# The start of an attention kernel: q and k positions as row part plus column part, x loaded first, idle products in the first gaps

## The chip, the cores and the metric

The kernel runs on one NeuronCore of one Trainium2 chip. The metric is the time of one execution on the device, in microseconds, as a median of several runs. A core has five engines with queues of their own: PE (TensorE, matrix products into PSUM), DVE (VectorE), ACT (ScalarE), POOL (GpSimd) and SP (SyncE, here only a queue of transfers). They run side by side and wait for one another through semaphores. 16 DMA engines move data between memory and SBUF.

## The reference, cut to what matters

The input x is 8 images of 128 channels and 48 x 48 = 2304 positions. Two layers follow each other. The first is a causal attention over the positions of the group-normalised x; the second a full attention over the same tokens, and a feed-forward recurrence. The change lies in the projections of the first layer:

```python
pe = jnp.broadcast_to(_pos_embeddings(S)[None], (B, 2 * EMB, S, S))
x0 = jnp.concatenate([x, pe], axis=1).reshape(B, C + 2 * EMB, N)     # C = 128, EMB = 16, N = 2304
q = lrelu(jnp.einsum('kc,bcn->bkn', Wq, x0) + bq[None, :, None])
k = lrelu(jnp.einsum('kc,bcn->bkn', Wk, x0) + bk[None, :, None])
v = lrelu(jnp.einsum('vc,bcn->bvn', Wv, x0) + bv[None, :, None])
attn = jnp.einsum('bkn,bkm->bnm', q, k) / jnp.sqrt(jnp.float32(Kdim))
# ... causal mask, softmax, times v; then x + this, layer norm, full attention, feed-forward
```

The 32 position channels are the same for all images. 16 of them depend on the row of the image alone and 16 on its column alone (`px`, `py` in `_pos_embeddings`). So W applied to them, plus the bias, is one fixed table of 128 x 2304 for each of q, k and v, and for each position a sum of a term by row and a term by column.

## The kernel before

All arithmetic is float32. The 2304 positions are cut into six chunks of QC = 384. A chunk n of an image is projected so: DVE normalises x (`xn`), PE multiplies by the three weights (`pj`), DVE adds the position table (`z`) and takes the leaky relu (`q`, `k`, `vT`), and reduces q and k to their largest magnitudes (a bound for the softmax). The position table `pb` of a chunk is made in the first image: PE multiplies the 33 position rows (32 channels and ones) by their weights, ACT copies the result from PSUM, and it is stored to memory (`posb_d`), from where later uses load it. In the first image chunks 0 and 1 are used straight from where they are made, chunks 2 to 5 are loaded back.

The engines' orders are fixed by the program. Chains of steps (`st.add`) are put between the attention products by a small model of the engines' times in the program: `tick` runs the steps that it holds ready, `advance` and `finish` force a chain to a step. The start and the projections:

```python
load_x(0, 3)                        # three transfers of 128x768 on the SP queue
...
wT = apool.tile([P, 3, P], F32, tag="wT", name="wT")
pe_sb = [gpool.tile([P, N // 2], F32, tag="g", name=f"pe_{h}") for h in range(2)]
wpT = tpool.tile([P, N // 2], F32, tag="t", name="wpT")[:, : 3 * P].rearrange("p (j c) -> p j c", j=3)
nc.scalar.dma_start(wpT[: NPE + 1], w_pos)
nc.scalar.dma_start(pe_sb[0][: NPE + 1, :], pe[:, : N // 2])
nc.scalar.dma_start(wT, w_qkv)
nc.sync.dma_start(pe_sb[1][: NPE + 1, :], pe[:, N // 2 :])
nc.sync.dma_start(w1, w_ffn)
...
def positions(n, j):                # table of chunk n for q, k, v (j = 0, 1, 2)
    if j == 0:
        if n < 2:
            pos[0, n] = made[n] = pbp.tile([P, 3, QC], F32, tag="pb", name=f"pb_0_{n}")
        else:
            made[n] = tpool.tile([P, 3 * QC], F32, tag="t", name=f"pb_0_{n}").rearrange("p (j c) -> p j c", j=3)
    pe_c = pe_sb[n // (NQ // 2)][: NPE + 1, ts(n % (NQ // 2), QC)]
    ps = psum_s(f"pb_{n}_{j}")
    if j < 2:
        nc.tensor.matmul(ps[:, :QC], wpT[: NPE + 1, j, :], pe_c, start=True, stop=True)
    else:
        for m in range(0, QC, P):
            nc.tensor.matmul(ps[:, ds(m, P)], pe_c[:, ds(m, P)], wpT[: NPE + 1, j, :], start=True, stop=True)
    nc.scalar.copy(made[n][:, j, :], ps[:, :QC])
    if j == 2:
        nc.sync.dma_start(posb_d[:, n], made[n])
...
def project(b, n):
    def normed():
        if n > 1:
            st.finish(projected[b, n - 2])
        if (b, n) in pos_loads:
            st.finish(pos_loads[b, n])
        c["pb"] = pos.pop((b, n))
        ...
        nc.vector.tensor_scalar(c["xn"], xbuf[b][:, cols], mg, rs, ALU.subtract, ALU.mult)
    def part(j):
        def f():
            ps = psum_s(f"pj_{b}_{n}_{j}")
            ...                     # q, k: one product of 384 columns; v: three of 128
            z = chunk_tile("z", f"z_{b}_{n}_{j}")
            nc.vector.tensor_add(z, ps[:, :QC], c["pb"][:, j, :])
            ...
            nc.vector.scalar_tensor_tensor(dst, z, 0.01, z, ALU.mult, ALU.max)
            if j == 2:
                for i in range(2):
                    nc.vector.tensor_reduce(
                        largest[b][:, i, n : n + 1], c[i], AX.X, ALU.max, apply_absolute_value=True
                    )
                load_positions(*divmod(b * NQ + n + 2, NQ))
                if n + 1 < EARLY:
                    project(b, n + 1)
    steps = [(normed, 0.0, [("DVE", 0.75)])]
    steps += [(part(j), QC * US, [("DVE", 0.0 if j < 2 else 4.5)]) for j in range(3)]
...
idle(psum_s("idle"), 12)            # 12 products of 128 columns that nobody reads
for j in range(3):
    positions(0, j)
gn = st.add(group_norm(0))          # statistics (DVE), mean and variance over groups (PE, DVE), root (POOL)
st.advance(gn, 2)
positions(1, 0)
st.finish(gn)
for j in range(1, 3):
    positions(1, j)
project(0, 0)
making = st.add([(partial(positions, n, j), QC * US, [("ACT", 0.5)]) for n in range(2, NQ) for j in range(3)], 6.0)
```

After that the attention products follow: for each query chunk j and key block m a score `s` (keys as weights, 384 columns or less), its exponential `p` on ACT (the block on the diagonal masked by POOL), and three scores later its product with v into `o`, while DVE adds p up into `acc`. `psum_s` has four buffers, `tpool` and `pbp` two each.

Of the kernel before, what the change touches and what calls it, by code (L numbers as in the profile page):

```python
# [21 lines left out]
EMB = 16  # L22
# [10 lines left out]
def position_rows(side):  # L33
# [13 lines left out]
    return np.ascontiguousarray(np.concatenate([px, py, ones], axis=0).reshape(NPE + 1, side * side))  # L47

# [556 lines left out]
def fast_path(ctx: ExitStack, tc: tile.TileContext, x, pe, w_ffn, out, x_tok, w_qkv, w_pos, v_t, gamma_beta, flag):  # L605
# [58 lines left out]
    with ExitStack() as actx:  # L664
# [69 lines left out]
        wpT = tpool.tile([P, N // 2], F32, tag="t", name="wpT")[:, : 3 * P].rearrange("p (j c) -> p j c", j=3)  # L734
        nc.scalar.dma_start(wpT[: NPE + 1], w_pos)
        nc.scalar.dma_start(pe_sb[0][: NPE + 1, :], pe[:, : N // 2])
        nc.scalar.dma_start(wT, w_qkv)
        nc.sync.dma_start(pe_sb[1][: NPE + 1, :], pe[:, N // 2 :])
# [4 lines left out]
        def ffn_weights():  # L743
# [4 lines left out]
            nc.vector.tensor_scalar(w1, w1, s, None, ALU.subtract)  # L748
            tp = psum_t("tp_ffn")
# [68 lines left out]
        keys, vals, queries, largest, projected = {}, {}, {}, {}, {}  # L818

        pos, pos_loads, made = {}, {}, {}  # L820

        def positions(n, j):

            if j == 0:
                if n < 2:
                    pos[0, n] = made[n] = pbp.tile([P, 3, QC], F32, tag="pb", name=f"pb_0_{n}")
                else:
                    made[n] = tpool.tile([P, 3 * QC], F32, tag="t", name=f"pb_0_{n}").rearrange("p (j c) -> p j c", j=3)
            pe_c = pe_sb[n // (NQ // 2)][: NPE + 1, ts(n % (NQ // 2), QC)]
            ps = psum_s(f"pb_{n}_{j}")  # L830
            if j < 2:
                nc.tensor.matmul(ps[:, :QC], wpT[: NPE + 1, j, :], pe_c, start=True, stop=True)  # L832
            else:
                for m in range(0, QC, P):
                    nc.tensor.matmul(ps[:, ds(m, P)], pe_c[:, ds(m, P)], wpT[: NPE + 1, j, :], start=True, stop=True)
            nc.scalar.copy(made[n][:, j, :], ps[:, :QC])
            if j == 2:
                nc.sync.dma_start(posb_d[:, n], made[n])

        def load_positions(b, n):  # L840
            def f():
                if b == 0:
                    st.advance(making, 3 * (n - 1))
# [3 lines left out]
            if b < B:  # L847
                pos_loads[b, n] = st.add([(f, 0.0, [])], st.free["DVE"] - st.now)

        def project(b, n):  # L850
# [4 lines left out]
            def normed():  # L855
                if n > 1:
                    st.finish(projected[b, n - 2])
                if (b, n) in pos_loads:
                    st.finish(pos_loads[b, n])
                c["pb"] = pos.pop((b, n))  # L860
# [8 lines left out]
            def part(j):  # L869
                def f():  # L870
# [15 lines left out]
                    if j == 2:  # L886
                        for i in range(2):
                            nc.vector.tensor_reduce(
                                largest[b][:, i, n : n + 1], c[i], AX.X, ALU.max, apply_absolute_value=True
# [743 lines left out]
```

## Time and profile before

| | |
|---|---|
| time, median of 3 runs | 1772.9 us (1772.55 to 1773.56) |
| span of the profiled execution | 1772.5 us |
| instructions | 22223 |
| moved by DMA | 262.00 MB, 148 GB/s on average |

A page of the profile gives the busy time of each engine (PEld is PE's weight load, which overlaps PE), the chain of work that ended last, and groups of instructions by line. An answer of the trace gives single instructions in order of time: when each began, how long it took, how long its engine had been idle before it and what released it. A float32 product appears in the records as two instructions (x2 for one product, x6 for three). In a product's operands the first number is of rows times columns of the weights: `33*128` is a position product, which has 33 rows, `128*128` one that uses the whole array. Idle time of an engine costs nothing as long as another engine sets the pace at that moment.

### The profile page before, as it was taken

Reading aid. Unit: us, or ns where it says so; the run is one execution under the profiler, and the core shown is the slowest. Engines: PE = TensorE matmul, PEld = TensorE weight load, DVE = VectorE, ACT = ScalarE, POOL = GpSimd, SP = SyncE. Lnnn points to the kernel's source line nnn. Section 1 sums busy time; section 2 is a strip of 40 time slices with the busy share of each in tenths; the row PEclk is TensorE's granted clock in tenths of the full one; section 3 lists DMA queues with packets and bytes.
Section 4 is the critical chain, followed back from the end, with each engine's and each line's share of the span. In section 5 each row is a group of like instructions: output and inputs, shape, how many; then the busy total and the mean of one; then the engine's idle time right before and its main releaser. Section 6 shows DMA issues by size and latency. Waiting matters only on the chain.

```text
span 1772.5 us, 22223 instructions
## 1 busy us (share of the span) xinstructions
PE 1742.7 (98%) x6231; PEld 1093.2 (62%) x6231; DVE 1302.8 (74%) x3363; ACT 764.8 (43%) x1842; POOL 195.2 (11%) x303
## 2 busy tenths in 40 slices
PE   8999999999999999999999999999999999999996
PEld 5666566665666566665666656665666656665565
DVE  4868668876887668786687767876687866877467
ACT  2344434443345434444344433454344543444455
POOL 1110011100110001100111001100011001110006
PEclk8999999999999999999999999999999999999998
DMA  4405672257533584156732575335941468116768
GB/s 140 138 23 187 182 204 94 87 184 188 145 103 128 159 226 141 34 176 182 200 99 80 188 192 152 106 111 161 237 129 50 160 183 214 45 65 198 194 211 216
DMA packets 206056, 262.00 MB, mean 148 GB/s; under 512 B 90113, under 2 KB 175010, under 8 KB 205412
## 3 DMA queue, kind: packets, MB, share of 16 engines
q1 hardware_dynamic: 204972, 257.47, 49.4%
q0 software_dynamic: 720, 2.62, 1.0%
q8 instruction: 52, 0.85, 0.2%
q14 instruction: 80, 0.66, 0.1%
q10 hardware_dynamic: 232, 0.40, 0.1%
HBM read 150.24 MB, written 110.17 MB: 147 GB/s over the span
## 4 chain that ended last, share of the span: by engine, by line
PE 96%; DMA 1%; DVE 1%; ACT 0%; issue 0%; SPq 0%; POOL 0%; ACTq 0%; POOLq 0%; DVEq 0%
PE o L1228 18%; PE s L1214 18%; PE s L1013 17%; PE o L1024 17%; PE o L1224 13%; PE pj L874 4%; PE pj L877 2%; PE z L1547 2%; PE wx L1320 2%; PE of_t L934 1%; PE tb L934 1%; PE pb L832 0%; DMA x<-in_x_dram 0%; PE dn L1072 0%; PE ts L1259 0%
## 5 line engine op out<-in xcount | busy, mean ns | idle before, releaser
L1216 ACT ACTIVATE p<-s,shift 128x384 f32<-128x384 f32 x504 | 292.4, 580 | 479.7 <-PE s L1214 464.2
L1015 ACT ACTIVATE p<-s 128x384 f32<-128x384 f32 (+2 forms) x504 | 231.8, 460 | 424.8 <-PE s L1013 377.5
L1214 PE MATMUL s<-xh 128*128 128x384 f32 x1008 | 410.4, 489 | 0.0
L1228 PE MATMUL o<-p,xhT 128*128 128x384 f32 x1008 | 404.1, 488 | 5.9 <-ACT p L1216 5.9
L1013 PE MATMUL s<-q,k 128*128 128x384 f32 (+2 forms) x1008 | 381.5, 460 | 0.2 <-DVE k L884 0.2
L1024 PE MATMUL o<-p,vT 128*128 128x384 f32 (+2 forms) x1008 | 377.4, 456 | 0.0
L1224 PE MATMUL o<-g,xhT 128*128 128x384 f32 x720 | 281.3, 488 | 1.1 <-DMA g<-e 1.1
L1228 PEld LDWEIGHTS o<-p,xhT 128*128 128x128 f32 x1008 | 188.9, 190 | 133.8 <-ACT p L1216 10.5
L1024 PEld LDWEIGHTS o<-p,vT 128*128 128x128 f32 x1008 | 188.8, 190 | 114.7 <-issue 0.6
L1214 PEld LDWEIGHTS s<-xh 128*128 128x128 f32 x1008 | 186.2, 190 | 115.3
L1013 PEld LDWEIGHTS s<-q,k 128*128 128x128 f32 x1008 | 182.6, 191 | 97.3 <-issue 1.0
L1039 DVE TENSOR_TENSOR acc<-acc,p 128x384 f32<-128x384 f32 (+2 forms) x408 | 208.8, 512 | 33.4 <-POOL p L1018 8.7
L1177 DVE STREAM_TRANSPOSE t<-p 128x384 f32<-128x384 f32 x360 | 187.3, 550 | 37.6 <-ACT p L1216 32.8
L1224 PEld LDWEIGHTS o<-g,xhT 128*128 128x128 f32 x720 | 133.2, 190 | 83.7 <-DMA g<-e 1.3
L1185 DVE TENSOR_REDUCE tsum<-t 128x12 f32<-128x1152 f32 x120 | 162.3, 1353 | 4.2
L879 DVE TENSOR_TENSOR z<-pj,pb 128x384 f32<-128x384 f32 x144 | 78.8, 547 | 108.8 <-PE pj L874 92.4
L1018 POOL TENSOR_TENSOR p<-p,triu 128x128 f32<-128x128 f32 x144 | 72.5, 505 | 606.2 <-ACT p L1015 475.2
L1294 POOL TENSOR_TENSOR roots<-ve_f,mhalf 128x3 f32<-128x3 f32 x48 | 40.7, 849 | 521.8 <-DVE ve_f L918 521.8
L1216 ACT ACTIVATION_READ_ACCUMULATOR p<-s,shift 128x1 f32 x504 | 97.2, 193 | 0.0
L874 PE MATMUL pj<-xn,wT 128*128 128x384 f32 x192 | 79.7, 500 | 1.4 <-DVE xn L867 1.4
L924 POOL TENSOR_TENSOR rs_c<-ve_c,mhalf 128x3 f32<-128x3 f32 x48 | 45.1, 939 | 216.2 <-DVE ve_c L918 213.6
L1321 DVE TENSOR_TENSOR scale<-wx,scale 128x384 f32<-128x384 f32 x46 | 25.4, 551 | 56.1 <-PE wx L1320 50.3
(264 smaller groups left out, 1485.6 us busy)
## 6 DMA issues: line engine op xcount, KB each, us to landing
e<-t SPq DMA_DIRECT2D x120, 576.0 KB
g<-e SPq DMA_DIRECT2D x480, 144.0 KB
pb<-posb_d SPq DMA_DIRECT2D x46, 576.0 KB
t1t<-in_x_tok_dram SPq DMA_DIRECT2D x48, 192.0 KB
t_d<-tt SPq DMA_DIRECT2D x184, 48.0 KB
t2x<-t_d SPq DMA_DIRECT2D x46, 192.0 KB
scale<-rs SPq DMA_DIRECT2D x46, 192.0 KB
x<-in_x_dram SPq DMA_DIRECT2D x14, 576.0 KB
```

What stands on the lines that cost most here:

```text
L874: nc.tensor.matmul(ps[:, :QC], wT[:, j, :], xn, start=True, stop=True)
L879: nc.vector.tensor_add(z, ps[:, :QC], c["pb"][:, j, :])
L1013: nc.tensor.matmul(s[:, off:QC], keys[b][:, ts(m, P)], queries[b, j][:, off:], start=True, stop=True)
L1015: nc.scalar.activation(p[:, off:], s[:, off:QC], AF.Exp, scale=SCALE)
L1024: nc.tensor.matmul(o[:, off:QC], vals[b][:, ts(m, P)], p[:, off:], start=first, stop=last)
L1039: nc.vector.tensor_add(a[:, off:], a[:, off:], p[:, off:])
L1177: nc.vector.transpose(t[:, :, :, g, :].rearrange("p b j r -> p j b r"), p.rearrange("p (j b r) -> p j b r", j=QB, b=R))
L1185: nc.vector.tensor_reduce(self.tsum[j][:, n - j - 1, :], t.rearrange("p b j m r -> p (b j) (m r)"), AX.X, ALU.add)
L1214: nc.tensor.matmul(s[:, :QC], xh[:, ts(m, P)], xh[:, ts(j, QC)], start=True, stop=True)
L1216: nc.scalar.activation(p, s[:, :QC], AF.Exp, bias=shift, accum_out=self.rows[:, m, j : j + 1])
L1224: nc.tensor.matmul(out_ap, xhT[:, QB * i + g, :], p, start=first, stop=last)
L1228: nc.tensor.matmul(o[:, :QC], xhT[:, what[1], :], p, start=first, stop=last)
```

## The change

The term by row and the term by column are made once for q and k (two products of 96 columns, copied by ACT). POOL adds them for every position of a chunk, with two broadcast operands, so that PE and ACT no longer make these two thirds of the table. The third for v, which needs the positions as rows, is made as before. In the first image every chunk is used where it is made; the store to memory stays, for the later images. x comes ahead of the large weight and position loads: on the ACT queue only two small loads are left, and the rest stand behind x on the SP queue. Idle products, 9, 4 and 5 of them, stand on PE where it waits for x and for the two steps of the statistics, to keep its clock up. The two maxima of a chunk become a chain of their own, and the preparation of a feed-forward weight is cut in two steps and moves from 30 to 60 us of the program's model of time. The core of the diff (cut: the new argument `pe_rc` in signatures and inputs):

```diff
@@
     py = np.broadcast_to(t[:, None, :], (EMB, side, side))
 ...
     return np.ascontiguousarray(np.concatenate([px, py, ones], axis=0).reshape(NPE + 1, side * side))
+def position_parts(side):
+    rows = position_rows(side)
+    parts = np.zeros((NPE + 1, 2, side), np.float32)
+    parts[:EMB, 0], parts[NPE, 0] = rows[:EMB, ::side], 1.0
+    parts[EMB:NPE, 1] = rows[EMB:NPE, :side]
+    return parts
 ...
 @with_exitstack
@@
 ...
         pe_sb = [gpool.tile([P, N // 2], F32, tag="g", name=f"pe_{h}") for h in range(2)]
-        wpT = tpool.tile([P, N // 2], F32, tag="t", name="wpT")[:, : 3 * P].rearrange("p (j c) -> p j c", j=3)
+        SIDE = pe_rc.shape[-1]
+        rcs = gpool.tile([P, N // 2], F32, tag="g", name="rcs")
+        rc_sb = rcs[:, : 2 * SIDE]
+        wpT = rcs[:, 6 * SIDE : 6 * SIDE + 3 * P].rearrange("p (j c) -> p j c", j=3)
         nc.scalar.dma_start(wpT[: NPE + 1], w_pos)
-        nc.scalar.dma_start(pe_sb[0][: NPE + 1, :], pe[:, : N // 2])
-        nc.scalar.dma_start(wT, w_qkv)
-        nc.sync.dma_start(pe_sb[1][: NPE + 1, :], pe[:, N // 2 :])
+        nc.scalar.dma_start(rc_sb[: NPE + 1, :], pe_rc.rearrange("k i s -> k (i s)"))
+        nc.sync.dma_start(wT, w_qkv)
+        for h in range(2):
+            nc.sync.dma_start(pe_sb[h][: NPE + 1, :], pe[:, ts(h, N // 2)])
         nc.sync.dma_start(w1, w_ffn)
 ...
-        def ffn_weights():
+        def ffn_centred():
 ...
             nc.vector.tensor_scalar(w1, w1, s, None, ALU.subtract)
+        def ffn_turned():
             tp = psum_t("tp_ffn")
 ...
             nc.vector.tensor_copy(w1T, tp[:, 0:P])
@@
             return [(part1, 0.0, [("DVE", 3.6)]), (part2, 0.15, [("DVE", 0.6)]), (part3, 0.15, [("DVE", 0.15), ("POOL", 0.9)])]
 ...
-        keys, vals, queries, largest, projected = {}, {}, {}, {}, {}
-        pos, pos_loads, made = {}, {}, {}
+        keys, vals, queries, largest, projected, ends = {}, {}, {}, {}, {}, {}
+        pos, pos_loads, made, making, parts = {}, {}, {}, {}, [0] * NQ
+        rc = rcs[:, 2 * SIDE : 6 * SIDE].rearrange("p (j s) -> p j s", j=2)
+        assert QC % SIDE == 0
+        def position_sums():
+            ps = psum_s("pb_rc")
+            for j in range(2):
+                nc.tensor.matmul(
+                    ps[:, ts(j, 2 * SIDE)], wpT[: NPE + 1, j, :], rc_sb[: NPE + 1, :], start=True, stop=True
+                )
+            nc.scalar.copy(rcs[:, 2 * SIDE : 6 * SIDE], ps[:, : 4 * SIDE])
 ...
-            if j == 0:
+            if n not in made:
                 if n < 2:
-                    pos[0, n] = made[n] = pbp.tile([P, 3, QC], F32, tag="pb", name=f"pb_0_{n}")
+                    made[n] = pbp.tile([P, 3, QC], F32, tag="pb", name=f"pb_0_{n}")
                 else:
                     made[n] = tpool.tile([P, 3 * QC], F32, tag="t", name=f"pb_0_{n}").rearrange("p (j c) -> p j c", j=3)
-            pe_c = pe_sb[n // (NQ // 2)][: NPE + 1, ts(n % (NQ // 2), QC)]
-            ps = psum_s(f"pb_{n}_{j}")
             if j < 2:
-                nc.tensor.matmul(ps[:, :QC], wpT[: NPE + 1, j, :], pe_c, start=True, stop=True)
+                k = QC // SIDE
+                nc.gpsimd.tensor_add(
+                    made[n][:, j, :].rearrange("p (i s) -> p i s", s=SIDE),
+                    rc[:, j, ts(n, k)].unsqueeze(2).to_broadcast([P, k, SIDE]),
+                    rc[:, j, SIDE:].unsqueeze(1).to_broadcast([P, k, SIDE]),
+                )
             else:
+                pe_c = pe_sb[n // (NQ // 2)][: NPE + 1, ts(n % (NQ // 2), QC)]
+                ps = psum_s(f"pb_{n}_{j}")
                 for m in range(0, QC, P):
                     nc.tensor.matmul(ps[:, ds(m, P)], pe_c[:, ds(m, P)], wpT[: NPE + 1, j, :], start=True, stop=True)
-            nc.scalar.copy(made[n][:, j, :], ps[:, :QC])
-            if j == 2:
+                nc.scalar.copy(made[n][:, j, :], ps[:, :QC])
+            parts[n] += 1
+            if parts[n] == 3:
                 nc.sync.dma_start(posb_d[:, n], made[n])
 ...
             def f():
-                if b == 0:
-                    st.advance(making, 3 * (n - 1))
                 pos[b, n] = pbp.tile([P, 3, QC], F32, tag="pb", name=f"pb_{b}_{n}")
 ...
-            if b < B:
+            if 0 < b < B:
                 pos_loads[b, n] = st.add([(f, 0.0, [])], st.free["DVE"] - st.now)
 ...
         def project(b, n):
@@
 ...
                 if n > 1:
-                    st.finish(projected[b, n - 2])
+                    st.advance(projected[b, n - 2], 4)
+                    st.advance(ends[b, n - 2], 1)
                 if (b, n) in pos_loads:
                     st.finish(pos_loads[b, n])
-                c["pb"] = pos.pop((b, n))
+                if b == 0 and n:
+                    st.advance(making[n], 1 if n < 4 else 3)
+                c["pb"] = pos.pop((b, n)) if b else made[n]
                 if n == 0:
 ...
                     vals[b] = big.tile([P, N], F32, tag="vT", name=f"vT_{b}")
@@
                     nc.vector.scalar_tensor_tensor(dst, z, 0.01, z, ALU.mult, ALU.max)
 ...
                     if j == 2:
-                        for i in range(2):
-                            nc.vector.tensor_reduce(
-                                largest[b][:, i, n : n + 1], c[i], AX.X, ALU.max, apply_absolute_value=True
-                            )
+                        ends[b, n] = st.add([(extremes, 0.0, [("DVE", 1.1)])], 6.0)
+                        if b == 0 and 4 <= n + 2 < NQ:
+                            making[n + 2] = st.add([
+                                (partial(positions, n + 2, i), 0.0 if i < 2 else QC * US, [("POOL", 1.0) if i < 2 else ("ACT", 0.5)])
+                                for i in (2, 0, 1)
+                            ], 0.0)
                         load_positions(*divmod(b * NQ + n + 2, NQ))
 ...
                             project(b, n + 1)
@@
 ...
+            def extremes():
+                for i in range(2):
+                    nc.vector.tensor_reduce(largest[b][:, i, n : n + 1], c[i], AX.X, ALU.max, apply_absolute_value=True)
             steps = [(normed, 0.0, [("DVE", 0.75)])]
-            steps += [(part(j), QC * US, [("DVE", 0.0 if j < 2 else 4.5)]) for j in range(3)]
+            steps += [(part(j), QC * US, [("DVE", 0.0 if j < 2 else 3.4)]) for j in range(3)]
             c["chain"] = projected[b, n] = st.add(steps)
 ...
         def bounds(b):
@@
                     if j + EARLY < NQ:
 ...
                     if j == NQ - 1:
+                        for n in range(NQ):
+                            st.advance(ends[b, n], 1)
                         bounds(b)
 ...
                 s = psum_s(f"s_{b}_{j}_{m}")
@@
                 ], max(at, st.free["DVE"]) + 0.2 - st.now)
 ...
         norm_chain = {}
-        st.add([(ffn_weights, 0.3, [("DVE", 0.5)])], 30.0)
+        st.add([(ffn_centred, 0.0, [("DVE", 1.4)]), (ffn_turned, 0.12, [("DVE", 0.2)])], 60.0)
         def idle(tp, n):
 ...
         idle(psum_s("idle"), 12)
-        for j in range(3):
+        position_sums()
+        for j in range(2):
             positions(0, j)
+        idle(psum_s("idle_x"), 9)
         gn = st.add(group_norm(0))
         st.advance(gn, 2)
-        positions(1, 0)
+        idle(psum_s("idle_m"), 4)
         st.finish(gn)
-        for j in range(1, 3):
-            positions(1, j)
+        idle(psum_s("idle_v"), 5)
         project(0, 0)
-        making = st.add([(partial(positions, n, j), QC * US, [("ACT", 0.5)]) for n in range(2, NQ) for j in range(3)], 6.0)
+        st.advance(projected[0, 0], 1)
+        for n in range(1, 4):
+            for j in range(2):
+                positions(n, j)
+        st.advance(projected[0, 0], 3)
+        positions(0, 2)
+        making.update({n: st.add([(partial(positions, n, 2), QC * US, [("ACT", 0.5)])], 1.0) for n in range(1, 4)})
 ...
```

More of the change, by code (lines that the diff above doesn't have):

```diff
@@ L604, in fast_path @@
 @with_exitstack
-def fast_path(ctx: ExitStack, tc: tile.TileContext, x, pe, w_ffn, out, x_tok, w_qkv, w_pos, v_t, gamma_beta, flag):
+def fast_path(ctx: ExitStack, tc: tile.TileContext, x, pe, w_ffn, out, x_tok, w_qkv, w_pos, pe_rc, v_t, gamma_beta, flag):
     nc = tc.nc
@@ L1618 @@
         "w_pos": np.stack([np.vstack([i[:, C:].T, inputs[f"L0_conv_b{n}"][None]]) for i, n in zip(w, "qkv")], axis=1),
+        "pe_rc": position_parts(H),
         "v_t": inputs["L1_ffn_V"].T,
```

## The prediction

> **What bounds the kernel now.** I read three views in this order: the busy table and the chain of the page, the busy time by stretch, and the timeline of the first 62 us.
>
> ```profile
> PE 1742.7 (98%) x6231; PEld 1093.2 (62%) x6231; DVE 1302.8 (74%) x3363; ACT 764.8 (43%) x1842; POOL 195.2 (11%) x303
> PE 96%; DMA 1%; DVE 1%; ACT 0%; issue 0%; SPq 0%; POOL 0%; ACTq 0%; POOLq 0%; DVEq 0%
> ```
>
> PE (TensorE) is busy 98% of the span and is 96% of the chain that ended last. So a microsecond counts if PE work vanishes, if PE stops idling, or if it runs at its full clock instead of half. Where is PE not at its peak?
>
> ```profile
> 0.00:50.00 50.00, 43.51 (x156) 28.23 (x157) 26.09 (x59) 13.12 (x27) 8.94 (x34) 0.86 0.40 136
> 50.00:100.00 50.00, 50.00 (x189) 32.20 (x189) 41.93 (x114) 19.05 (x41) 7.79 (x13) 1.00 0.37 119
> 200.00:300.00 100.00, 100.00 (x367) 63.52 (x368) 76.30 (x200) 37.47 (x80) 11.51 (x20) 1.00 0.63 174
> 1600.00:1700.00 100.00, 96.76 (x327) 57.79 (x326) 52.85 (x142) 41.65 (x106) 4.24 (x5) 1.00 0.68 181
> 1700.00:1772.00 72.00, 56.80 (x285) 47.87 (x284) 55.21 (x98) 44.01 (x112) 29.45 (x29) 0.92 0.76 233
> ```
>
> Columns: the stretch, its length, busy us of PE, PEld, DVE, ACT and POOL with counts, granted PE clock, DMA share, GB/s. From 50 to 1600 us PE idles 0.63 us per batch at most; only the first 50 us (6.5 us idle, mean clock 0.86) and the last 80 have slack. The change touches the first. It is read in the timeline (start, duration, engine, line, operation; in brackets the idle time before it and what ended it):
>
> ```profile
> 7.14 1.52 PE L832 MATMUL pb<-pe,wpT 33*128 33x384 f32 x4 [0.37 <-DMA pe<-position_rows]
> 9.20 1.02 DVE L791 BATCH_NORM_STATS2 gn_st<-x 128x6 f32<-128x384 f32 x2 [0.96 <-DMA x<-in_x_dram]
> 10.72 0.56 PE L799 MATMUL gn_m<-gn_mv,grp 128*128 128x1 f32 x2 [1.39 <-DVE gn_mv L793]
> 13.30 1.64 PE L832 MATMUL pb<-pe,wpT 33*128 33x384 f32 x2
> 14.73 1.48 PE L835 MATMUL pb<-wpT,pe 33*128 33x128 f32 x6
> 16.15 2.93 PE L874 MATMUL pj<-xn,wT 128*128 128x384 f32 x4
> 20.41 0.88 PE L1013 MATMUL s<-q,k 128*128 128x384 f32 x2 [0.19 <-DVE k L884]
> 30.09 0.43 PE L750 MATMUL tp_ffn<-ident,w 128*128 128x128 f32 x1 [1.50 <-DVE w L748]
> 31.60 1.49 PE L1013 MATMUL s<-q,k 128*128 128x384 f32 x2
> 35.98 0.56 DVE L879 TENSOR_TENSOR z<-pj,pb 128x384 f32<-128x384 f32 x1 [5.13 <-DMA pb<-posb_d]
> 48.09 0.91 PE L874 MATMUL pj<-xn,wT 128*128 128x384 f32 x2 [1.44 <-DVE xn L867]
> 62.42 0.81 PE L1013 MATMUL s<-q,k 128*128 128x384 f32 x2
> ```
>
> Four things are to be seen. The last third of x reaches DVE at 9.20. Then position products (pb) stand between the group statistics and the first projection: xn is ready at 14.73, its product starts at 16.15. A projection pair takes 2.93 us instead of 2 x 0.645 us (the steady spacing): the clock is halved. DVE, whose projections feed everything, loses 5.13 us until a position tile has gone to memory and back. The row at 62.42 is the first score of query chunk 3; from there on both kernels have the same PE work but for one transpose (0.2 us). So **the start of that score is my yardstick**.
>
> [...] from the clock by microsecond I place the switches near 9.7 (down), 19.9 (up), 30.2 (down) and 33.6 (up), multiples of 3.41 apart. [...] here about 1.6 us of idle in one (28.6 to 30.1) was enough, while 1.44 us (46.6 to 48.1, split between two windows) was not. [...] The trace has two-input POOL operations of 128x128 at 505 ns and of 128x512, strided, at 1871 ns; a 128x384 one lies between, my estimate is 1.1 us. [...] the POOL 128x128 product takes 0.45 us, and 0.65 beside DVE's xn at 28.99. [...] So the 0.40 MB on the ACT queue slow x, which lies on the SP queue; by microsecond 392 GB/s fall to 281 to 304 while they mix.
>
> **The change part by part.**
>
> *x first.* Until x was there, some 1.75 MB had moved; x with the two small loads left on the ACT queue is 1.24 MB. The cumulated traffic of before reaches that at 6.2 us; with 0.8 us from data to DVE, the last third starts at 7.0 instead of 9.20. Statistics 1.02 and aggregate 0.35: ready at 8.4 instead of 10.6.
>
> *Idle products.* 12 as before, at half clock to 6.8; the two row/column products (96 columns) 0.35; then 9 idle ones of 128 columns, 9 x 0.213 = 1.9 us, to 9.0. So the statistics product starts at 9.0, held 0.6 us by idle work, against 10.72. Four idle products (0.85) fill the wait for DVE; the variance product starts at 10.15 against 12.78, as no 1.64 us pair stands before it. DVE, POOL (0.57) and xn (0.48) follow as before: xn at 11.95, first projection at 12.05 against 16.15: **4.1 us**. The clock should stay full, so both projections take 1.3 and not 2.6 us.
>
> *Positions on POOL.* On PE 6912 columns of pb become 2496 (192 of them the parts), 7.4 us at 600 columns/us; 2304 idle columns are added, 3.8 us, in gaps. Eight POOL adds for chunks 0 to 3 take 9 us, done near 19, ahead of their use by DVE (z of chunk 1 at 19.6). The round trip through memory is gone, and with it the 5.13 us.
>
> *What then sets the pace: DVE.* Per chunk: three z and three lrelu at about 0.58, two maxima at 0.5, xn at 0.47, together 5 us. Walking both orders with these durations:
> chunk 0: z at 12.95, k ready 15.3, first score 15.4 (20.41 before), maxima and xn of chunk 1 ready at 17.95. PE fills in with three position products for v, and projects chunk 1 at 18.7 to 20.65.
> chunk 1: z 19.6, k 21.95, score of chunk 1 at 22.05 (31.60 before), after a PE gap of 1.4. v, maxima, xn of chunk 3: 24.55; PE waits 1.3.
> chunks 3 and 2: q of 3 at 26.7, xn of 2 at 27.15, sums 27.8, z of 2 from 28.15, v of 2 at 31.7, maxima 32.6, k and v of 3 at 35.0, xn of chunk 4 at 35.5. PE has only 3.2 us of work meanwhile, then its order puts a projection of chunk 4 next: **a new PE gap from about 31.1 to 35.6, 4.5 us**.
> From there PE has 17.0 us of work to the yardstick (projections 2.56, scores and outputs 13.8, positions 0.64): 52.65 at full clock. Against 62.42 that is -9.8.
>
> Corrections: a gap of 4.5 us halves the clock; with the window phase of before PE works at half speed from 35.6 to about 40.4 and loses 2.4. The two gaps of 1.3 to 1.4 may halve it once more, where DVE is the limit: +0.4 as a mean. Contention of POOL and DVE: +0.5, guessed. The moved transpose +0.2. Sum: -9.8 + 2.4 + 0.4 + 0.5 + 0.2 = **-6.3 us**.
>
> *Later batches.* Splitting the maxima into a chain of their own and taking 3.4 instead of 4.5 us for them in the schedule moves projections a few products earlier in every batch. The work is the same, DVE has 20 to 30% slack there, so I put 0 +- 2 us.
>
> **The rivals.**
> 1. *Nothing arrives*: what DVE lets go early is all waited for at chunk 4, and the cold clock takes the rest: 1771 to 1773. For it: the 4.5 us gap. Against it: DVE's own list is shortened by the 5.13 us, and it starts 4 us earlier.
> 2. *POOL becomes the bound*: adds at 2 us instead of 1.1 would end near 24.5, holding the masked p of chunk 0 and the z of chunk 3, and could delay the root that xn waits for: about 2 us lost, 1768 to 1769. For it: the strided 1871 ns. Against: xn of chunk 3 is not there before 24.55 anyway.
> 3. *All of it arrives*: the clock recovers at once and the gap is shorter: 1762 to 1763.
> 4. *Later batches wait*: half a microsecond more in each of seven batches would give 3.5 back: 1770. The 0.63 us that one product per batch waits for ACT may as well go.
>
> **Range and chances.** 1772.9 - 6.3 = 1766.6. Rivals 1, 2 and 4 on one side and 3 on the other span 1762 to 1771. A change of 2% would be 35 us; everything before the yardstick is 62 us and nothing later loses or gains work, so I give each side 1%.
>
> **What would show it right or wrong.** x at DVE near 7.0; first projection near 12 in 1.3 us at clock 1.0; first score near 15.4; POOL adds near 1.1 us; no DVE wait for a position load; a PE gap of some 4.5 us ended by xn just before 36, with half clock after it; the yardstick near 56; after it a constant shift. It would be wrong if POOL adds take over 2 us, if the idle products leave the clock at half, or if the shift drifts from batch to batch.

## The result, and the profile after

| | before | after |
|---|---|---|
| median, us | 1773.23 (1772.55 to 1773.68, 4 runs) | 1780.25 (1778.09 to 1781.03, 4 runs) |
| ratio, 95% interval | | 1.0038 [1.0021, 1.0055] |
| span of the profiled execution, us | 1772.5 | 1779.3 |

The kernel became slower by 0.2 to 0.6%, where 1766.6 us had been predicted. The busy table and the chain of waits of the kernel after:

```profile
PE 1737.8 (98%) x6247; PEld 1091.2 (61%) x6247; DVE 1299.2 (73%) x3363; ACT 757.3 (43%) x1831; POOL 216.3 (12%) x315
PE 94%; DMA 3%; DVE 1%; issue 1%; SPq 0%; ACT 0%; POOL 0%; ACTq 0%; DVEq 0%; POOLq 0%
```

PE is busy for 4.9 us less than before (1742.7), and still the end is later: transfers, 1% of the chain before, are 3% of it now, and that is where to look. By stretch (columns as before: busy us of PE, PEld, DVE, ACT, POOL, then PE's clock, DMA share, GB/s):

```profile
0.00:50.00 50.00, 41.35 (x200) 30.62 (x201) 30.66 (x63) 10.01 (x21) 19.36 (x46) 0.97 0.35 125
50.00:100.00 50.00, 50.00 (x186) 31.86 (x185) 41.66 (x120) 19.39 (x43) 8.65 (x15) 1.00 0.28 88
200.00:300.00 100.00, 98.79 (x366) 62.73 (x366) 75.68 (x209) 37.76 (x79) 13.53 (x21) 1.00 0.63 167
1000.00:1100.00 100.00, 96.99 (x339) 59.46 (x338) 64.30 (x169) 35.15 (x84) 7.42 (x13) 0.98 0.69 185
```

The first row is what was wanted: mean clock 0.97 instead of 0.86. The news is in the third and fourth: 1.21 us of idle PE between 200 and 300 us, where before had none, and 3.01 us (0.63 in before) and a clock below 1 between 1000 and 1100. The timeline of the start, which answers to the one shown of before:

```profile
6.71 1.02 DVE L807 BATCH_NORM_STATS2 gn_st<-x 128x6 f32<-128x384 f32 x2 [0.46 <-DMA x<-in_x_dram]
7.30 2.27 PE L1441 MATMUL idle_x<-ident 128*128 128x128 f32 x18
7.77 0.32 DVE L809 BATCH_NORM_AGGREGATE gn_mv<-gn_st 128x2 f32<-128x36 f32 x1
9.41 0.28 PE L815 MATMUL gn_m<-gn_mv,grp 128*128 128x1 f32 x2
11.64 5.50 POOL L859 TENSOR_TENSOR pb<-rcs 128x384 f32<-128x384 f32 x6
11.69 0.98 DVE L902 TENSOR_SCALAR xn<-x,gn_mg,gn_rs 128x384 f32<-128x384 f32 x1 [0.69 <-POOL gn_rs L671]
12.78 1.53 PE L909 MATMUL pj<-xn,wT 128*128 128x384 f32 x4 [0.75 <-issue]
16.51 0.91 PE L1056 MATMUL s<-q,k 128*128 128x384 f32 x2 [0.47 <-DVE k L919]
22.92 0.88 PE L1056 MATMUL s<-q,k 128*128 128x384 f32 x2
36.74 1.37 PE L909 MATMUL pj<-xn,wT 128*128 128x384 f32 x2 [3.20 <-DVE xn L902]
55.92 0.81 PE L1056 MATMUL s<-q,k 128*128 128x384 f32 x2
```

The first projection pair takes 1.53 us at full clock, the first score comes at 16.51 (20.41 before), the gap before the projection of chunk 4 is there (3.20 us), and my yardstick, the first score of query chunk 3, starts at 55.92 instead of 62.42: 6.5 us won.

These microseconds are lost again, image by image. Setting the same score of the full attention (the second layer of an image) of both traces side by side, after minus before:

| image | 0 | 1 | 2 | 3 | 4 | 5 | 6 | 7 | end |
|---|---|---|---|---|---|---|---|---|---|
| shift, us | -6.4 | -4.9 | -3.2 | -1.4 | -1.5 | +3.1 | +4.5 | +6.3 | +6.8 |

Within an image the shift doesn't move; it jumps at six of the seven joints, where the full attention of one image runs beside the projections of the next. The list of PE's waits of after names what is new:

```profile
PE o L1267 <- DMA g<-e: 9.8, 7, 2.4
...
PE pj L909 <- DVE xn L902: 5.0, 2, 3.2
```

(Columns: us in total, times, longest.) In before the same wait is there once, 1.07 us at 1683. `e` is a chunk of attention weights that DVE has transposed and the SP queue has stored to memory; `g` is the same chunk loaded back by the same queue in another order (four transfers of 144 KB), and that PE multiplies. Six of the seven waits lie at the joints, 1.15 to 2.37 us each, 9.3 together. Behind the longest, PE also runs at half clock for 3.4 us (1.7 us lost), and each of the other five jumps is some 0.25 us more than its wait. That is 9.3 + 1.7 + 1.25, some 12.2 of the 12.7 us between the shifts of -6.4 and +6.3.

Why is `g` late? The queue of SP at the first joint, first of before and then of after (start, duration, line, transfer, count):

```profile
232.04 3.69 SPq L1148 DMA_DIRECT2D g<-e  x8
235.84 0.38 SPq L845 DMA_DIRECT2D pb<-posb_d  x1
236.60 1.73 SPq L1148 DMA_DIRECT2D g<-e  x4
```

```profile
224.83 1.73 SPq L1191 DMA_DIRECT2D g<-e  x4
226.66 0.38 SPq L877 DMA_DIRECT2D pb<-posb_d  x1
227.62 1.73 SPq L1191 DMA_DIRECT2D g<-e  x4
```

Before issues two loads of `g` and then the position load of chunk 3 of the next image, 576 KB. After issues one load of `g`, then the 576 KB, and the second `g` (pair 3,5 of chunks, `g_3_5` below) behind them. The chain of waits of after at this place:

```profile
228.45 0.42 SPq L1191
228.87 0.04 issue
228.92 7.28 DMA g<-e
236.20 0.04 issue
236.25 0.91 PE o L1267 x2
```

From its issue the load takes 7.28 us to land. The 16 DMA engines have no room: their share from 228 to 236 us is 0.97 to 1.10 at 220 to 274 GB/s, so at this rate the 576 KB alone are over 2 us. PE's product waits 1.21 us for it.

### The profile page after: what moved, and what is told of

The parts are those of the page before. It is cut to its first block, busy times and chain, and to the rows that moved or that the text cites. A ratio compares the mean times of both kernels' runs of the same rounds, so it can differ in the third digit from the quotient of the medians.

```text
span 1779.3 us, 22220 instructions
## 1 busy us (share of the span) xinstructions
PE 1737.8 (98%) x6247; PEld 1091.2 (61%) x6247; DVE 1299.2 (73%) x3363; ACT 757.3 (43%) x1831; POOL 216.3 (12%) x315
## 2 busy tenths in 40 slices
DMA packets 205524, 259.65 MB, mean 146 GB/s; under 512 B 90093, under 2 KB 174990, under 8 KB 204880
## 4 chain that ended last, share of the span: by engine, by line
PE 94%; DMA 3%; DVE 1%; issue 1%; SPq 0%; ACT 0%; POOL 0%; ACTq 0%; DVEq 0%; POOLq 0%
PE s L1257 18%; PE o L1271 18%; PE s L1056 17%; PE o L1067 17%; PE o L1267 11%; PE pj L909 3%; DMA g<-e 2%; PE wx L1363 2%; PE z L1597 2%; PE pj L912 1%; PE tb L975 1%; PE of_t L975 1%; SPq L1191 0%; DVE z L914 0%; DMA t2x<-t_d 0%
## 5 line engine op out<-in xcount | busy, mean ns | idle before, releaser
L1061 POOL TENSOR_TENSOR p<-p,triu 128x128 f32<-128x128 f32 x144 | 77.5, 540 | 506.9 <-ACT p L1058 505.6
L1324 DVE SCALAR_TENSOR_TENSOR t<-of_t,ri,t1t 128x128 f32<-128x128 f32 x144 | 41.5, 344 | 43.3 <-PE of_t L975 43.3
```

## The experiments

Theory A: the start gained what was predicted, and the loss comes from the order of two loads on one queue, a position load now standing ahead of `g_3_5` in seven images. Rival B: it comes from the order of the products and of DVE's work, which the new chain of maxima also moves (buffers come free later, PE waits elsewhere). Times below are medians with their ranges; each ratio is to runs of the kernel before on the same chip (their medians were 1774.35, 1774.16, 1773.98 and 1774.59 us in the four sets below).

**e1, e2: which part loses.** e1 keeps the new start and gives the chains of images 1 to 7 their old form; e2 is the kernel before with only those chains changed.

```diff
 e1, against after
                 if n > 1:
-                    st.advance(projected[b, n - 2], 4)
-                    st.advance(ends[b, n - 2], 1)
+                    if b:
+                        st.finish(projected[b, n - 2])
+                    else: ...                      # as after
                     if j == 2:
-                        ends[b, n] = st.add([(extremes, 0.0, [("DVE", 1.1)])], 6.0)
+                        if b:
+                            extremes()
+                        else: ...                  # as after
-            steps += [(part(j), QC * US, [("DVE", 0.0 if j < 2 else 3.4)]) for j in range(3)]
+            steps += [(part(j), QC * US, [("DVE", 0.0 if j < 2 else 4.5 if b else 3.4)]) for j in range(3)]
```

Expected of e1:

> The start of the change as it is, the chains of images 1 to 7 as in the kernel before (from the first full attention on, the order of every engine is that of before). Theory A (the 13 us are lost where two images meet, because the new chains put the 576 KB position load of chunk 3 ahead of the load of g_3_5 on the SP queue) and theory B (they are lost there because the new chains move projections ahead of the products that free the g buffers) both expect the start gain to stay: 6.4 us under before, 1766 to 1767. If the losses came from the start itself (an earlier start meeting other transfers), it would be 1779 as the changed kernel.

Expected of e2:

> The kernel before, with only the chains of images 1 to 7 as in the change. A and B: no gain at the start and the whole loss later, 1773 + 13 = 1784 to 1788. If the two parts are not independent: 1773 to 1780.

e1: 1771.61 us (1769.63 to 1775.63, 21 runs), ratio 0.9986 [0.9980, 0.9993]. e2: 1784.94 (1780.62 to 1793.91, 6 runs), ratio 1.0068 [1.0046, 1.0091]. The loss belongs to the later images' chains, as both theories say. e1 won only 2.7 us on the kernel before (1774.35): in its profile the shift of image 0 is -4.9 instead of -6.4 (taken up below), 1.2 us are lost at two joints where small waits for `g` are left, and 2.3 us more after the first score of image 7.

**e3, e4: only the queue.** e3 is the kernel after, with the position load of chunk 3 issued right behind that of `g_3_5`; each compute engine keeps the order of after, and on the SP queue seven pairs are swapped. e4 is the reverse: e1 with the position load put ahead.

```diff
 e3, against after
+        behind = []
         def load_positions(b, n):
-            def f():
+            def issue():
                 pos[b, n] = pbp.tile([P, 3, QC], F32, tag="pb", name=f"pb_{b}_{n}")
...
+            def f():
+                if n == 3:
+                    behind.append(issue)
+                else:
+                    issue()
...                                    # at the end of load() of g:
+                if (i, j) == (3, NQ - 1) and behind:
+                    behind.pop()()
 e4, against e1, at the start of load() of g
+                if (i, j) == (3, NQ - 1) and (self.b + 1, 3) in pos_loads:
+                    st.advance(pos_loads[self.b + 1, 3], 1)
```

Expected of e3:

> The changed kernel with one pair of transfers per image swapped on the SP queue: the position load of chunk 3 stands behind the load of g_3_5. The orders of PE, DVE, ACT and POOL are those of the changed kernel. A: the waits of PE for g vanish, with 9.8 us and the 1.7 us of the half clock behind one of them, 1767 to 1770. B: nothing changes, 1778 to 1781.

Expected of e4:

> The start-only kernel with the opposite swap: the position load of chunk 3 ahead of the load of g_3_5, all other orders kept. A: PE waits for g in seven images, 1 to 2 us each, 1774 to 1780. B: same as the start-only kernel, 1766 to 1767.

e3: 1769.78 us (1766.89 to 1771.03, 7 runs), ratio 0.9970 [0.9959, 0.9981]. Swapping seven loads is worth 0.7% and turns the loss into a gain. e4: 1780.50 (1778.40 to 1783.48, 5 runs), ratio 1.0038 [1.0025, 1.0051], 8.9 us slower than e1. B falls in both directions; A stands. The waits of PE, first of e3, then of e4:

```profile
PE o L1279 <- DMA g<-e: 0.8, 1, 0.8
```

```profile
PE o L1275 <- DMA g<-e: 7.3, 8, 1.9
```

In e3 the shift is -6.7 at image 0 and -6.6 at image 7. The first joint of e3, the queue and then PE (busy time by stretch):

```profile
225.06 4.00 SPq L1201 DMA_DIRECT2D g<-e  x8
229.16 0.38 SPq L879 DMA_DIRECT2D pb<-posb_d  x1
```

```profile
232.00:234.00 2.00, 2.00 (x8) 1.19 (x7) 1.85 (x9) 0.00 (x0) 0.00 (x0) 1.00 0.95 362
234.00:236.00 2.00, 2.00 (x9) 1.29 (x8) 1.46 (x4) 0.56 (x2) 0.46 (x1) 1.00 1.04 252
```

The DMA engines are as full as in after, where PE is busy for 1.04 of these last 2 us; here for all 2.00. Both kernels move 259.65 MB; only what comes first has changed. Nor is `g_3_5` asked for sooner: its first issue is at 227.34 us here and at 227.62 in after, and the two executions are 0.3 us apart by then (-6.7 and -6.4). What matters is what stands ahead of it.

**e5, e6, e7: the terms of the start**, each against e3, which ran again beside them.

```diff
 e5
-        idle(psum_s("idle_x"), 9)
-        idle(psum_s("idle_m"), 4)
-        idle(psum_s("idle_v"), 5)
 e6
-        nc.sync.dma_start(wT, w_qkv)
-        for h in range(2):
-            nc.sync.dma_start(pe_sb[h][: NPE + 1, :], pe[:, ts(h, N // 2)])
+        nc.scalar.dma_start(pe_sb[0][: NPE + 1, :], pe[:, : N // 2])
+        nc.scalar.dma_start(wT, w_qkv)
+        nc.sync.dma_start(pe_sb[1][: NPE + 1, :], pe[:, N // 2 :])
 e7
-                    st.advance(ends[b, n - 2], 1)
+                    if b or n > 3:
+                        st.advance(ends[b, n - 2 if b else n - 4], 1)
-                        ends[b, n] = st.add([(extremes, 0.0, [("DVE", 1.1)])], 6.0)
+                        ends[b, n] = st.add([(extremes, 0.0, [("DVE", 1.1)])], 6.0 if b else 26.0)
```

Expected of e3 again:

> The changed kernel with the position load of chunk 3 behind the load of g_3_5 once more, as the yardstick on this chip for the three variants of its start: 1767 to 1771 us, first score of query chunk 3 near 56 us, the shift of some -6.6 us constant through all images.

Expected of e5, e6 and e7:

> As the yardstick, with the 18 new idle products at the first gaps (idle_x, idle_m, idle_v) taken out and nothing else. If they are what keeps the clock up: half clock in one or two windows between about 8 and 17 us, the first projection pair in 2.6 us instead of 1.5, the two statistics products some 0.5 us earlier each; together the first score 0.5 to 1.5 us later and the time 0.5 to 2 us above the yardstick. If the wait for DVE hides it all (the rival): the first score within 0.3 us of the yardstick's and the same time, or even less by the 0.4 us that the statistics product no longer waits for idle ones.

> As the yardstick, with the loads of the position rows and of the projection weights put back on the ACT queue beside x, as in the kernel before; every compute engine keeps its order. If the loads that mix with x are what made x late (my step of 2.2 us): the last third of x at DVE near 8.5 to 9, xn and the first projection 1.5 to 2 us later, and the time 1 to 2 us above the yardstick. If x is bound by something else (the rival): x at DVE within 0.4 us of 6.7 and the same time.

> As the yardstick, with the maxima of the first image's chunks put off behind the normalization of the next chunks on DVE (later images keep their order), so that xn of chunk 4 is made sooner. If the 3.2 us gap ahead of the projection of chunk 4 and the half clock after it are a matter of DVE's order: the gap falls under 1.5 us, no half clock between 37 and 40, the yardstick score 1.5 to 4 us earlier and the time 1 to 3 us below the yardstick's. If DVE is simply full there (the rival): the gap turns up at another projection or score and the time is within 0.7 us.

The means product is `gn_m`, PE's first product of the group statistics; the shift is that of image 0, as in the table above.

| | median, us | ratio to before | means product at | first score | shift, image 0 |
|---|---|---|---|---|---|
| e3 again | 1768.34 (1768.19 to 1769.93, 5) | 0.9964 [0.9951, 0.9977] | 9.98 | 17.08 | -4.9 |
| e5 | 1772.35 (1770.73 to 1778.89, 14) | 0.9996 [0.9986, 1.0007] | 7.92 | 16.57 | -3.5 |
| e6 | 1770.82 (1765.92 to 1771.67, 6) | 0.9971 [0.9960, 0.9983] | 9.74 | 16.83 | -4.5 |
| e7 | 1769.87 (1767.27 to 1772.33, 8) | 0.9975 [0.9965, 0.9985] | 9.65 | 16.74 | -6.6 |

e5: the idle products are what keeps the kernel ahead of before, but not as expected. Without them the mean clock is 0.989 to 0.993 in all 14 executions, against 0.994 to 0.996 in e3 again. In the profiled one (1771.24 us, among the faster) the means product comes 1.2 to 2.1 us earlier (9.15 in e3, 9.41 in after, 9.98 in e3 again); the clock is half from 8.5 to 15.4 us, the projection pair takes 2.93 us, and at the first score the two effects cancel. The time lost lies later: half clock from 35.8 to 46.1, three windows of 3.4 us instead of one. That these three follow from the missing products is not shown: e11 below, which has 11 of the 18, has three there too. e6: the last third of x comes to DVE at 7.95, where the 13 profiles with x first have 6.27 to 7.48, and nothing follows from it, because the nine idle products hold the means product past that anyway. e7 doesn't close the gap before chunk 4 (3.35 us, 3.20 in e3 again), and the one before chunk 3 grows from 1.42 to 2.60: DVE is full there (busy 3.93 of the 4 us from 33 to 37), as the rival said. By its time e7 can't be told from e3 again.

**e8 to e11: the idle products, sized anew.** e8 has 2 instead of 9 products `idle_x`; e9 puts 9 and 20 of them into the gaps before the projections of chunks 3 and 4; e10 does both; e11 is e8 with the loads of e6.

```diff
 e9, in part(j)
                     ps = psum_s(f"pj_{b}_{n}_{j}")
+                    if b == 0 and j == 0 and n in (3, 4):
+                        idle(ps, 9 if n == 3 else 20)
```

> As e3, with 2 instead of 9 idle products ahead of the product of the group means; nothing else. In e3_again those 9 hold that product to 9.98 us, 1.3 us after DVE has its input. If they are a hold without a use: means product at 8.5 to 9.1, xn and first projection about 1 us earlier with the clock still full, first score near 16, time 0.5 to 1.5 us below e3. If they are needed for the clock (the rival): a half clock window between 9 and 17 us, the first projection pair in 2.5 to 2.9 us instead of 1.53, and the time equal to or above e3's.

> As e3, with 20 idle products put into the gap before the projection of chunk 4 and 9 into the one before the projection of chunk 3 (2.5 and 1.1 us at full clock). If the half clock behind the 3.2 us gap is caused by that gap: no half clock between 36 and 45 us, yardstick score 1.5 to 2 us earlier than e3 in a run with one half clock window there and more in one with two, time 1.5 to 3 us below e3, less spread. If the clock falls all the same or the idle products hold the projection (the rival): within 0.5 us of e3 or slower.

> Both: 2 idle products at the means, and the two gaps filled. If both effects are real and apart: the sum of the two, 2 to 4 us below e3, so 1764 to 1767 us, ratio to the kernel before near 0.995. If the 1 us won at the start is only waited for again at chunk 4 (DVE's list sets when xn of chunk 4 comes, and it starts 1 us earlier, so I doubt it): the same as with the gaps filled alone.

> As e8, with the loads of the position rows and projection weights back on the ACT queue beside x. In e6 the later x (7.95 against 6.7 to 7.3 us) was hidden behind the 9 idle products. With only 2 it should show: x last third at DVE near 8, means product near 9.5 to 9.8, first projection 0.7 to 1.3 us later than in e8, time 0.5 to 1.3 us above e8. If loading x first is worth nothing even then: the same time as e8 within 0.4 us.

e8 1768.49 us (0.9974 [0.9964, 0.9984]), e9 1768.97 (0.9966 [0.9953, 0.9979]), e10 1767.54 (0.9960 [0.9947, 0.9973]), e11 1770.43 (0.9976 [0.9968, 0.9984]): none can be told from e3. In e8 the means product starts at 8.95, ended by DVE, and the profiled execution shows no half clock from 9 to 44 us (its projection pair takes 1.53 us) and a shift of -8.3; but by their mean clocks (0.993 to 0.997) other executions have, and the runs spread from 1766.62 to 1772.64. e9 was a mistake of size: an idle product takes 0.23 us and not 0.13, so that the 20 took 4.63 us and held the projection 1.3 us past its xn.

**Half clock without a gap.** In e3 again, with no gap, PE drops to half clock at 21.2 us. Its timeline there (PE only), and the stretch and its successor:

```profile
17.92 1.60 PE L868 MATMUL pb<-rcs,pe 33*128 33x128 f32 x12
19.45 0.70 PE L1066 MATMUL s<-q,k 128*128 128x256 f32 x2
20.08 0.93 PE L868 MATMUL pb<-rcs,pe 33*128 33x128 f32 x6
20.94 0.59 PE L1066 MATMUL s<-q,k 128*128 128x128 f32 x2
21.32 2.77 PE L919 MATMUL pj<-xn,wT 128*128 128x384 f32 x4
```

```profile
17.79:21.20 3.41, 3.41 (x23) 2.71 (x23) 1.65 (x4) 1.99 (x5) 0.91 (x2) 1.00 0.54 212
21.20:24.62 3.42, 3.42 (x10) 2.20 (x10) 1.53 (x3) 0.61 (x2) 0.46 (x1) 0.50 1.01 403
```

PE is busy for all 3.41 us of the first stretch, and the clock is 0.50 in the next. What differs is the tile: `33*128`, the position products for v use 33 of the 128 rows of the array, for 2.5 of the 3.4 us. That the rows matter for the clock was a guess. e14 makes these products over all 128 rows (the added rows are ones times zero weights, so the sums stay the same; six take 0.83 us instead of 0.93); e12 fills the gaps with 4 and 12 idle products; e13 is both.

```diff
 e14, against e3
+        for tile, value in ((wpT, 0.0), (pe_sb[0], 1.0), (pe_sb[1], 1.0)):
+            nc.vector.memset(tile, value)
-                pe_c = pe_sb[n // (NQ // 2)][: NPE + 1, ts(n % (NQ // 2), QC)]
+                pe_c = pe_sb[n // (NQ // 2)][:, ts(n % (NQ // 2), QC)]
-    ... pe_c[:, ds(m, P)], wpT[: NPE + 1, j, :] ...
+    ... pe_c[:, ds(m, P)], wpT[:, j, :] ...
```

> As e3, with 4 idle products ahead of the projection of chunk 3 and 12 ahead of that of chunk 4 (0.23 us each: 0.9 and 2.8 us, inside the gaps of 1.4 to 1.8 and 3.2). If the 3.2 us gap is what halves the clock between 36 and 45 us: no half clock there, first score of query chunk 3 some 1.5 us earlier than in a run of e3 with the same windows before, time 1 to 2 us below e3. If the 33-row products bring a half-clock window between 18 and 26 us all the same, as in e9 and e10, the gain shrinks to nothing in those executions.

> As e12, with the position products for v over 128 rows instead of 33 (the 95 added rows are ones times zero weights, so the sums stay the same; three memsets on DVE before x arrives). If the clock counts rows: no half-clock window from 7 us to the tail in any execution, mean granted clock 0.996 to 0.997, shift at the first scores of query chunk 3 near -8.3 us, time 1764.5 to 1767 us with little spread. If rows don't matter: the same as e12.

> As e3, with the position products over 128 rows and nothing else. If the clock counts rows: no half clock between 17 and 26 us in any phase of the windows, and one window only (3.4 us) behind the 3.2 us gap instead of one to three; shift -6.5 to -8.3, time 1766 to 1768.5 us. If rows don't matter: as e3 (1768 to 1770 us), half clock behind windows without a gap in some executions.

| | median, us | ratio to before | mean clock of the executions | shift, image 0 |
|---|---|---|---|---|
| e12 | 1767.08 (1765.55 to 1768.77, 5) | 0.9952 [0.9938, 0.9966] | 0.996 to 0.997 | -6.5 |
| e13 | 1765.40 (1764.79 to 1767.69, 5) | 0.9948 [0.9934, 0.9962] | 0.996 to 0.997 | -9.7 |
| e14 | 1767.45 (1765.86 to 1767.96, 5) | 0.9955 [0.9942, 0.9969] | 0.995 to 0.997 | -8.1 |

In e14's profile the clock stays at 1.00 from 15.30 to 22.13 us, over and behind 1.8 us of position products with 128 rows (its lines are in the last section). By the mean clock of the profiled executions, 0.996 in e12 and e14 and 0.997 in e13, the first two may have one window of half clock more than e13: 3.41 us at half clock take 0.001 from the mean over 1765 us (an estimate, from rounded figures). Behind what it lies isn't shown. e13's profile is at full clock over its first 50 us (of its other executions one, 1767.69 us at a mean clock of 0.996 instead of 0.997, may have a window of half clock):

```profile
0.00:50.00 50.00, 44.24 (x244) 34.94 (x245) 36.43 (x73) 10.73 (x23) 21.39 (x49) 1.00 0.40 139
```

Mean clock 1.00 over the first 50 us (0.86 before, 0.97 after). e13 is the fastest kernel of the study, and beats both before and after; that it beats e12 and e14 its interval doesn't show.

## Why the prediction was wrong

- *Later batches.* This is the step that failed: "The work is the same, DVE has 20 to 30% slack there, so I put 0 +- 2 us." Measured: +13.2 us from image 0 to the end. The work was the same, but the step looked at PE and DVE only. The same edit moves the issue of a 576 KB load ahead of a load that PE waits for, on one queue, at a place where the DMA engines are full (a share of 0.97 to 1.10). e3 takes just that back, and the shift stays between -6.7 and -6.6 from image 0 to image 7. Rival 4 ("Later batches wait") had the direction but named no transfer, and its half microsecond per image was 1.15 to 2.37 plus a clock window. The order of the SP queue stands in the program before any run; the prediction weighs PE's products and DVE's slack only. Which of the chain's three edits (own chain, 3.4 instead of 4.5, order of `advance`) moves the load wasn't tried apart.
- *x first* and *idle products.* x at DVE was put at 7.0 and came at 6.71. But the means product came at 9.41 instead of 9.0, held 1.3 us by idle work and not 0.6 (DVE was ready at 8.09 instead of 8.4, and the nine idle products took 2.27 us instead of 1.9). The 12 idle products of before, put at half clock, took 5.17 us, 0.43 each, while its clock by microsecond reads 1.00 up to 9 us: what slowed them isn't shown. The 2.2 us put down to x first were counted from a late execution: the last third of x came at 9.20 in before, but at 8.31 in e2, which starts as before does, and the first third at 5.18 and 3.98. Why before's data were late is not explained. From 8.31 to the 6.27 to 7.48 of the profiles with x first it is 0.8 to 2.0 us. That the loads on the ACT queue slow x was an estimate from before's rate by microsecond; with them back, x came at 7.95 in e6 and 7.72 in e11, and nothing of it shows at the end.
- *First projection and score.* 12.05 and 15.4 were predicted, 12.78 and 16.51 measured. Beside the hold, DVE's xn takes 0.98 instead of 0.48 us and q's leaky relu 1.06 instead of 0.56 while POOL's adds run: together 1.0 us on the way to the first score, twice the guess for contention.
- *Positions on POOL.* 1.1 us per add was estimated, 0.83 is the median measured (0.82 to 1.14); done at 17.1 and not 19. No wait for a position load is left in the first image. Right, with a spare.
- *Gap before chunk 4.* 4.5 us predicted, 3.20 measured, ended by xn as said; one window of half clock behind it, 1.7 us instead of 2.4.
- *Sum.* Yardstick near 56, -6.3: measured 55.92, -6.5. The parts erred by up to 1.3 us and cancelled: that is luck. And the value is one draw: by the profiles the same start gave -4.9 in e1, e4 and e3 again, and -6.7 in e3 (e3 again has two windows of half clock, e3's mean clock of 0.97 over 50 us is that of one), and in e2 the yardstick of the old start itself came at 61.87 instead of 62.42. In the medians e3 won 4.6 us on before, and e3 again 5.8.
- "It would be wrong ... if the shift drifts from batch to batch": it drifted.

## What to carry to other kernels

When a change moves work between queues or merely shifts the model that orders them, lay every queue's order beside the old one, the transfer queue first: where the DMA engines were full, as here (a share of 0.97 to 1.10), a load of 576 KB put one place too early delayed the one behind it, and PE, its reader, by 1.15 to 2.37 us. A gain at the start is worth what is left of it at the end, so follow the shift of one repeated instruction from batch to batch. Put loads with slack behind loads with a waiting reader, and size filler work with its measured duration (an idle product took 0.23 us and not 0.13), or it holds what waits behind it.

## What the runs showed of the hardware

The switches of the clock lie multiples of 3.41 us apart (in before near 9.7, 19.9, 30.2 and 33.6 us), so time is cut here into windows of that length. What stood in them comes from the timelines, the clock from the busy time by stretch or from the duration of the products (a projection takes 0.81 us at full clock, 1.49 at half):

| kernel, window (us) | clock in it | no product, us | position products, us | clock after it |
|---|---|---|---|---|
| e8, 34.5 to 38.0 | full | 1.9 | 0 | full |
| after, 1071.2 to 1074.7 | full | 2.0 | 0 | half |
| e5, 32.4 to 35.8 | full | 2.4 | 0 | half |
| before, 26.8 to 30.2 | full | 1.5 | 1.4, 33 rows | half |
| before, 19.9 to 23.4 | full | 0.2 | 2.1, 33 rows | full |
| e6, 17.2 to 20.6 | full | 0 | 2.4, 33 rows | full |
| e3 again, 17.8 to 21.2 | full | 0 | 2.5, 33 rows | half |
| e9, 15.3 to 18.7 | full | 0.5 | 1.6, 33 rows | half |
| e14, 15.3 to 18.7 | full | 0.6 | 1.8, 128 rows | full |
| e5, 35.8 to 39.3 | half | 0.8 | 0 | half |
| e10, 18.4 to 21.8 | half | 0 | 1.6, 33 rows | half |
| after, 37.0 to 40.4 | half | 0 | 0.7, 33 rows | full |

First the pair that differs in the rows, e9 and then e14 (each time the window and the one after it), then the two windows nearest to each other in idle time with different clocks after them, e8 and after (columns as above):

```profile
15.25:18.66 3.41, 2.94 (x18) 2.00 (x16) 2.98 (x6) 1.24 (x3) 1.74 (x3) 1.00 0.43 173
18.66:22.08 3.42, 3.42 (x12) 2.46 (x11) 0.00 (x0) 1.35 (x4) 0.68 (x2) 0.50 0.86 338
15.30:18.72 3.42, 2.79 (x19) 2.47 (x20) 2.96 (x6) 1.47 (x4) 1.73 (x3) 1.00 0.43 172
18.72:22.13 3.41, 3.32 (x20) 2.49 (x19) 1.80 (x4) 0.98 (x3) 0.92 (x2) 1.00 0.97 381
```

```profile
34.54:37.95 3.41, 1.48 (x6) 0.98 (x6) 2.24 (x5) 0.00 (x0) 0.00 (x0) 1.00 0.68 231
1071.20:1074.60 3.40, 1.33 (x5) 1.01 (x6) 0.15 (x1) 0.00 (x0) 0.17 (x1) 1.00 1.11 230
```

In the windows at full clock without a 33-row product, the clock stayed after 0.6 us (e14) and 1.93 us (e8) without a product, and fell after 2.04 us (after) and 2.4 us (e5). So a window need not be empty for a fall. With 33-row products the order is not so plain: the clock fell behind 2.5 us of them without a gap (e3 again) and stayed behind 2.4 us of them without a gap (e6); gaps and 33-row products together were 2.1 us in e9, where it fell, and 2.3 us in before from 19.9, where it stayed. Nor did a window without a gap always bring the clock back: in e10, with 1.6 us of 33-row products, it stayed half, in after, with 0.7 us, it rose; and in e5 it stayed half behind 0.8 us without a product. In before from 26.8 us, 1.4 us of 33-row products lay beside the 1.5 us without a product (1.6 in the prediction): the idle time didn't stand alone there.

That the rows matter rests on e9 against e14 at 15.3 us: 1.6 us of products over 33 rows and 0.5 us without a product, then a clock of 0.50; 1.8 us over 128 rows and 0.6 us without a product, then 1.00. It is one window of one profile each, and e6 kept its clock with 33 rows: not a proof, and how rows would act on the clock isn't shown. The start of such a kernel is therefore not one number: e3 again has two windows of half clock, 1.7 us lost in each, and e3, the same kernel, a mean clock over its first 50 us that leaves room for one.

Two smaller ones. In after a broadcast add of 128x384 on POOL takes 0.83 us (median of 12), and some DVE operations beside it take about twice their time: xn 0.98 instead of 0.48 us, and the leaky relu 1.06 and 1.20 instead of 0.56. It isn't so each time: of the six leaky relus that overlap an add in after, four take 0.56 to 0.60 us, and some of the adds take 1.14 instead. In before the prediction had one case to go by, a POOL product of 0.65 us beside xn instead of 0.45. And a load of `g` behind a position load, 576 KB each, took 7.28 us from its last issue to landing.
